# A four-layer residual chain whose instruction order is a table of numbers: the numbers of the prologue and of blocks 0 to 13 are replaced

## The chip, the cores and the metric

The kernel runs on one core of one Trainium2 chip. The time is device microseconds of one launch; a kernel is given as the median of its runs. A profiled execution also gives a span, from the first to the last instruction, and a trace of every instruction.

## The reference

The input x is 128 sequences of 64 tokens with 256 features. Four layers are added to it, one after the other, each steered by conditions of the sequence:

```
x = x + L0(x, cond)     # modulated linear, 16-head self-attention with q = k = v, modulated linear
x = x + L1(x, cond)     # per-sequence down projection, relu, up projection, plus its input
x = x + L2(x, ids ...)  # layer norms with gathered gains, small MLPs, a 6*256 -> 256 -> 256 MLP, layer norm
x = x + L3(x, cond)     # a rank-30 weight decoded per sequence: out = x @ (U V) + bias
```

In L0 the keys are `kx = x @ w_mod.T`, the scores `kx kx.T / 4` for each head, `A = softmax(scores)` and `out = A @ kx`. In L2 the first gain is gathered by a token's id out of 250 rows, the others out of 5 or 3 rows, and `_mlp_ln` is a silu MLP with a layer norm behind it. All of it is float32.

## The kernel before

**Tiling.** The 8192 tokens are cut into 16 blocks of 512 (8 sequences). A block runs through all four layers; within the attention it is worked in two pairs of 256 tokens (`pair_attention`), and elsewhere in four tiles of 128. A prologue makes what all blocks share: the style vectors and demodulations (L722, L734, L735, L743), the down and up conditions, the decoded weights `uu` (matmuls at L851, VectorE or ScalarE behind them at L866 and L858), the weights `w_t`, `w_s`, `w_h`, `w_x`, and the three small MLPs of L2 (the shared helper at L629 issues their matmuls).

**Order.** No loop sets the order of the instructions. Every operation is first noted with what it reads and writes (`Plan.op`), under its block (-1 for the prologue) and its running number in that block, counted from 0. `Plan.order` then emits them: of the operations whose predecessors are out and whose buffers are free it takes the one with the smallest number. The number is the block's start, 881500 times the block, plus an entry of the table `TURNS[block]`. Buffers of one kind are handed out in the order in which they were noted, except the four PSUM banks ("bank") and the one four-bank PSUM buffer ("sc"), which go to whoever comes first. So the tables alone set the order in the queues of TensorE, VectorE, ScalarE, GpSimd and SyncE, each of which runs strictly in the order it was given.

```
    def turns(blk, k):
        return max(blk, 0) * TURN + tables[blk][k]
...
    while plan.noted[-1] + 1 < SPINS:
        spin()
```

**Spins.** `SPINS` is the length of table -1. The prologue notes 231 operations; the rest of the table's entries are `spin`, a bf16 matmul of zeros into a bank that nobody reads (L638).

**The steps that are spoken of below**, with their entries in a block's table:

- 17 and 18 (GpSimd, L1097) scale x by the style; 19 to 22 are the gathers of gains, an indirect DMA each, issued from GpSimd (L1112).
- 31 and 59 (TensorE, L1191) are the key products of the two pairs, 8 matmuls of 128x256 each; VectorE multiplies them out (L1202) and GpSimd adds a bias (L1213).
- 34 to 62: VectorE transposes the keys (L1228, and L1245 for the values), ScalarE makes `kR` (L1237, entries 32 and 60), TensorE turns the values (L1256, entries 34 and 62).
- 36, 64 in block 0, and 40, 68 in the later ones: the scores (L1276), 128 small matmuls and 128 weight loads; they need `kR` and the buffer "sc". VectorE takes their maxima (L1289), TensorE subtracts them (L1350), ScalarE exponentiates (L1364).
- 48, 76 in block 0, and 52, 80 in the later ones: the results (L1381), again 128 small matmuls with 128 loads.
- L1418, L1155: the turn of the result and the output projection. L1573 and L1591: the down and up products. L1688: turns for the normalised x. L1738: the large MLP, 8 groups of matmuls of 128x512 for each half. L1785: the second MLP layer.
- In the prologue, entries 177 and 181 are the second and third of the MLPs' first products (L629), each for one half of the features.

**DMA.** Loads and stores are issued from SyncE's queue; a store or a load that reads what another engine has just made holds up every load behind it there.

Of the kernel before, what the change touches and what calls it, by code (L numbers as in the profile page):

```python
# [66 lines left out]
class Plan:  # L67
# [98 lines left out]
    -652225 -652207 -501809 -501797 549383 103302 97834 98988 -85347 -290328 36942 -280951 36928 -327022 -327038  # L166
    -295554 -34519 99192 -93568 76051 -488538 -331376 250663 -320110 311371 -544127 -297616 224193 -331358 437866
    369544 404601 258598 475097 427655 312750 413551 304934 313766 312765 477842 -325751 561445 451452 460137 631735
    653018 914561 435225 761948 708892 413433 313012 683513 477384 477856 415801 449087 706556 405021 840033 397966
    837121 677936 790176 413437 1085501 936816 1219990 374944 1127563 -488523 52290 364768 79632 -329221 31806 69353  # L170
    -302391 37394 74911 -302398 -135690 103317 253823 37375 113108 263257 -19093 -550935 407657 459732 455180 631946
    302035 554215 632190 302064 695445 435656 1285010 1313672 -271895 459095 641073 632445 439004 715974 662881
    443771 715988 735063 451708 763102 706553 455767 763114 790156 408270 1002127 1127290 1030643 1260783 1163421
    1039496 1260792 1322499 1326714 1592341 1603338 1296229 962570 1143817 400034 1095103 400034 1114596 1105723
    370540 1181851 589031 1073580 1215404 1215398 420508 1317621 426029 1244494 1155098 517782 411678 1318626
    1221030 487418 1289492 1063938 409314 1219811 414916 1426329 1505888 1316718 425996 578876 1307095 1544800
    1509955 1509945 1500478 1779993 1762953 1714110 1556735 1872029 1343778 1433951 1901071 1540726 1505870 1355549
    1749223 1065262 1886158 1894341 1920839 1713830 1294728 1463917 2023267 2025009 2024993 1769125 2080980 1991910
    1476886 1764730 2069423 1404270 2200384 1433935 1923896 1907021 2044892 1919551 2192488 1893429 2159446 1342047
    1346981 1402219 2313495 2045469 2494753 2285999 2271380 2543401 2525610 1728898 1728909 2630317 2592995 1746037  # L180
    2451743 1728921 2595973 1718576 1277644 2062908 2395255 316359 450207 16049267 16049281 14504150 -291503
    11290964 2389482 -291825 16049286 -291820 14522440 16049266 16053420 -320001 13567795 -410994 14513815 -361547
    15405911 16048186 16073369 -309973 14522440 16005249
    """,
    0: """
    -484581 84372 -652203 -35682 684863 1289506 1005368 578863 1258365 2419509 2111364 2061858 1597541 357479
    -327047 377451 733801 366553 -328204 806711 387288 365083 406034 1377907 1111313 1160718 1672215 -332266 56194
    404606 447219 455369 431572 -15187 267150 595783 567747 302041 312750 629212 662899 609068 653445 312737 466428
    715978 309121 309112 857128 436276 489161 370548 806701 1063944 1120732 641246 410676 725568 436305 410648
    709812 410662 609042 1119259 602370 436294 477217 820104 818673 1002143 818654 1083255 1103114 1063941 1120265  # L190
    1117581 1073560 1181852 1168792 409321 1262701 1205334 414910 1357801 1505886 426004 1063898 411662 1462748
    1518640 1230468 1433890 1749255 1749239 1431873 1872425 2190164 1919575 1872422 2174910 2278764 2321415 2384852
    2430654 2088493 2292286 2543835 2599889 2409496 1589520 2271367 2543830 2512135 1803634 1326310 2714126 1751071
    1758943 1758957 1758947 2523186 1589506 2427752 2206922 2711663 1788133 2711694 1788156 2575469 2528666 2544499
    2733360 2898539 2917556 2711682 2568763 2598822 2598852 2711679 2711696 2733311 2598849 2781651 2986041 2354176
    2409591 2568757 2598832 2711671 2711680 2733358 2733329 2733335 2985571 2986044 2476838 3049866 2529124 3019122
    3049851 2529112 3092405 3152898 3152886 2477574 3204028 3204039 2342116 2350219 3160743 3160731 2697860 3153889
    3310393 3353979 3296818 3367447 3109127 3394993 3420441 3762300 1336203 3409996 1469597
    """,
    1: """  # L200
    -394079 -394092 -482733 -425615 -297831 -337865 -325537 -299039 -482716 297196 735637 407985 -421370 1532404
    443756 1548772 1282128 -1264679 -1264697 916581 1275890 1398962 1806910 176525 220234 -35053 255915 516626
    953340 1101650 829819 -272447 -445206 -64857 -359383 -359389 244494 192909 345134 348760 345130 -367222 -461014
    348778 399333 182401 437115 -417743 -417760 535346 420908 265999 768088 829973 832612 837576 833713 675251
    992893 182426 -481464 -506569 -460994 -466571 450753 -394211 625417 462288 625425 618981 624383 413787 413768
    669870 343193 742774 770597 629993 403311 404542 576441 1104386 1135196 1129763 833262 576451 1171507 595405
    1281040 1289755 520725 1288546 1288527 1081797 1404289 982233 1509004 1472691 1546270 1619792 2137602 1717458
    880232 2135345 2272406 1286799 2320256 2356575 2322518 1460605 2544746 2443636 2180116 2356564 1460588 2544726
    2443622 2044761 2544726 2667741 2486731 2485304 2485318 2485298 2245174 2417516 2227520 2427513 2713637 2584615
    2732909 2598456 2420038 2515062 2444000 2464209 2891247 2903613 2544651 2550373 2576192 2608410 2732899 2803358  # L210
    2464175 2465276 2999349 3013321 2916210 2539226 2567809 2577443 2710725 2727178 2803374 2464189 2454008 2930134
    2862729 3001178 3086911 2483864 2483874 3086910 2483867 3104930 2787555 2777533 3153776 2867590 2867592 1986833
    3029354 2367123 2367108 1913805 2953463 3334225 3302746 3334216 3352156 3407259 3425296 3382877 3491141 471262
    3509343 449882
    """,
    2: """
    -506971 -506984 -473467 -51547 -995523 -772166 -1268595 -801997 -473451 -48533 -341685 -506980 -506979 -519158
    306888 -502791 1004205 -58852 -58870 589526 2052273 589554 1561323 -500303 35094 -350214 -59960 220156 325567
    197340 398256 -206237 108215 71820 160868 160862 187456 160866 -299085 267210 -360793 311626 281895 -319 304375
# [1800 lines left out]
```

## Time and profile before

| what | value |
|---|---|
| median of 9 runs | 822.09 us (817.21 to 828.91) |
| the profiled execution's own time | 822.83 us |
| its span | 821.1 us |
| mean granted TensorE clock | 0.982 |
| TensorE matmuls busy | 754.5 us (92%) |
| VectorE busy | 589.4 us (72%) |
| GpSimd busy | 565.6 us (69%) |
| ScalarE busy | 361.3 us (44%) |

The profiled execution is 1.7 us longer than its span and 0.7 us above the median of the runs. Busy times of an engine are sums over its instructions; the granted clock is the share of full speed that TensorE was given. An idle time is put down to what ended it: "DVE mr" is a VectorE instruction that wrote mr, "issue" means that the engine waited for nothing that the profile shows.

### The profile page before, as it was taken

The numbers are of one execution on the slowest core, as the hardware profiler recorded it, in microseconds if no ns is written. First come the engines' busy times: TensorE is split into PE (matmuls) and PEld (weight loads), VectorE is DVE, ScalarE is ACT, GpSimd is POOL, SyncE is SP. The second block draws the span as 40 slices with busy tenths as digits, with TensorE's granted clock in tenths as the row PEclk, the third lists the DMA queues.
The fourth block names the chain that finished last, engine by engine and source line by source line (L and its number), as shares of the span: only waits on it lengthen the run. The fifth ranks groups of instructions, "written<-read, shape, count | busy, mean of one in ns | idle before, by whom it ended". The sixth has DMA issues, their size and how long they took to land.

```text
span 821.1 us, 29440 instructions
## 1 busy us (share of the span) xinstructions
PE 754.5 (92%) x12839; PEld 489.8 (60%) x12843; DVE 589.4 (72%) x1320; ACT 361.3 (44%) x664; POOL 565.6 (69%) x544
## 2 busy tenths in 40 slices
PE   8778889999999999999999999999999989999695
PEld 6655655666666565666666665656566655655353
DVE  4747885967868696969687786869596876866435
ACT  1564345453536362544435353625355253444331
POOL 5453878395877878586869688795779586828243
PEclk9996999999999999999999999999999999999989
DMA  8776652234332234333433333342434232023001
GB/s 264 246 238 207 211 131 79 77 104 106 110 112 78 77 97 130 92 118 93 108 102 95 106 102 93 97 136 67 123 87 117 80 80 65 3 66 100 17 1 52
DMA packets 59297, 87.63 MB, mean 107 GB/s; under 512 B 6456, under 2 KB 42400, under 8 KB 59168
## 3 DMA queue, kind: packets, MB, share of 16 engines
q1 hardware_dynamic: 54048, 68.96, 28.7%
q0 software_dynamic: 5120, 16.78, 7.2%
q8 instruction: 101, 1.65, 0.9%
q14 instruction: 28, 0.23, 0.1%
HBM read 72.48 MB, written 13.24 MB: 104 GB/s over the span
## 4 chain that ended last, share of the span: by engine, by line
PE 60%; DVE 18%; POOL 8%; ACT 5%; issue 4%; DMA 4%; SPq 0%; DVEq 0%; POOLq 0%; ACTq 0%
PE bank L1738 23%; PE bank L1191 5%; PE bank L1785 5%; PE sc L1276 4%; DVE st L611 3%; PE bank L1688 3%; DVE mr L1289 3%; PE bank L1381 3%; PE bank L1155 2%; PE bank L629 2%; PE bank L1573 2%; PE bank L1591 1%; DVE bank L1162 1%; PE bank L1648 1%; PE bank L1823 1%
## 5 line engine op out<-in xcount | busy, mean ns | idle before, releaser
L1289 DVE TENSOR_REDUCE mr<-sc 128x16 f32<-128x1024 f32 x64 | 75.7, 1211 | 11.3 <-PE sc L1276 11.2
L1364 ACT ACTIVATE e<-sc 128x1024 f32<-128x1024 f32 x64 | 62.4, 1027 | 35.2 <-PE sc L1350 35.2
L1112 POOL DMA_INDIRECT pw<-in_pw,idx x64 | 65.3, 1021 | 16.0 <-issue 8.2
L1155 PE MATMUL bank<-osT,wo 128*128 128x512 f32 x128 | 63.8, 627 | 5.4 <-DVE osT L1425 5.1
L1191 PE MATMUL bank<-wk,xsT 128*128 128x256 f32 x256 | 62.1, 385 | 1.3 <-DVE uu L866 0.6
L1738 PE MATMUL bank<-uu,w_s 128*128 128x512 f32 x128 | 63.3, 597 | 0.0
L1237 ACT ACTIVATE kR<-kT,early 128x1024 f32<-128x1024 f32 x32 | 39.7, 1242 | 50.6 <-DVE kT L1228 50.6
L1738 PE MATMUL bank<-uu,w_t 128*128 128x512 f32 x128 | 61.3, 605 | 0.3 <-ACT uu L1655 0.2
L1738 PE MATMUL bank<-uu,w_h 128*128 128x512 f32 x128 | 61.4, 602 | 0.0
L1381 PEld LDWEIGHTS bank<-e,v 64*32 64x32 f32 x4096 | 45.0, 107 | 27.5 <-issue 23.4
L1276 PEld LDWEIGHTS sc<-kR,kT 20*64 20x64 f32 x4096 | 48.1, 132 | 20.5 <-ACT e L1364 8.2
L1738 PE MATMUL bank<-x2T,w_x 128*128 128x512 f32 x128 | 59.9, 593 | 0.0
L1381 PE MATMUL bank<-e,v 64*32 64x64 f32 x4096 | 52.5, 229 | 7.9 <-issue 7.7
L1785 PE MATMUL bank<-w,uu 128*128 128x256 f32 x240 | 55.8, 385 | 2.1 <-DVE uu L1758 2.0
L1276 PE MATMUL sc<-kR,kT 20*64 20x64 f32 x4096 | 53.2, 235 | 4.7 <-issue 1.9
L1191 PEld LDWEIGHTS bank<-wk,xsT 128*128 128x128 f32 x256 | 48.5, 196 | 12.7 <-issue 4.0
L1202 DVE TENSOR_TENSOR kxe<-bank,dmk 128x512 f32<-128x512 f32 x32 | 22.0, 688 | 44.2 <-PE bank L1191 38.6
L1693 ACT COPY uu<-bank 128x512 f32<-128x512 f32 x64 | 36.5, 587 | 38.6 <-PE bank L1688 38.4
L1129 POOL TENSOR_TENSOR wdn<-gdb,late 128x512 f32<-128x512 f32 x32 | 40.6, 1283 | 14.5 <-PE bank L1573 13.9
L1785 PEld LDWEIGHTS bank<-w,uu 128*128 128x128 f32 x240 | 44.3, 190 | 9.7 <-DVE uu L1758 4.0
L1228 DVE STREAM_TRANSPOSE kT<-kxe 128x512 f32<-128x512 f32 x64 | 42.1, 684 | 9.3 <-POOL kxe L1213 9.3
L1213 POOL TENSOR_TENSOR kxe<-kxe,kbr 128x512 f32<-128x512 f32 x32 | 41.0, 1282 | 11.0 <-DVE kxe L1202 10.7
(241 smaller groups left out, 1782.5 us busy)
## 6 DMA issues: line engine op xcount, KB each, us to landing
xT<-in_xT SPq DMA_DIRECT2D x32, 256.0 KB
gdb<-dgdb SPq DMA_DIRECT2D x16, 512.0 KB
ubb<-ugub SPq DMA_DIRECT2D x32, 256.0 KB
wup<-ugub SPq DMA_DIRECT2D x32, 256.0 KB
ids<-in_ids SPq DMA_DIRECT2D x16, 256.0 KB
ud<-uu SPq DMA_DIRECT2D x8, 512.0 KB
uT<-ud SPq DMA_DIRECT2D x16, 256.0 KB
dmk<-demod_k SPq DMA_DIRECT2D x60, 64.0 KB
```

The lines of the kernel that those rows point to most:

```text
L1112: lambda tl=tl, n=n: nc.gpsimd.indirect_dma_start(out=pw[tl // 2].t[:, tl % 2, :], out_offset=None, in_=a["pw"], in_offset=bass.IndirectOf ...
L1129: lambda w=w, dp=dp: nc.gpsimd.tensor_tensor(w(), gdb.t[:, :, 0:64], dp, ALU.mult),
L1155: nc.tensor.matmul(ps.t, owT[:, c, bass.ts(oc, 128)], osT.t[:, c, :], start=(c == 0), stop=(c == C - 1))
L1191: nc.tensor.matmul(ps.t[:, bass.ts(l, F)], xsT.t[:, c, mine2].rearrange("p (n l) -> p l n", l=2)[:, l, :], kwT[:, c, :], start=(c == 0), s ...
L1213: lambda: nc.gpsimd.tensor_tensor(kxe.t[:, :, :, 0:D], kxe.t[:, :, :, 0:D], heads(kinds["kbr"][0]).unsqueeze(1).to_broadcast([128, 2, H, D ...
L1228: lambda l=l: nc.vector.transpose(kT.t[:, l, :].rearrange("p (g h t) -> p h g t", h=H, t=QT), kxe.t[:, l, :, :]),
L1276: nc.tensor.matmul(sc.t[64 * c : 64 * c + 64, q, bass.ts(tg, 64)], cut(kT.t)[r, tg // 4, c, tg % 4, :], cut(kR.t)[r, tg // 4, c, tg % 4, : ...
L1289: lambda two=two: nc.vector.tensor_reduce(mr.t[:, two, :], sc.t[:, two, :].rearrange("p q (g n) -> p q g n", g=TG), AX.X, ALU.max),
L1364: lambda k=k: nc.scalar.activation(es[k].t, sc.t[:, 2 * k : 2 * k + 2, :], AF.Exp, scale=0.25),
L1381: nc.tensor.matmul(placed(pr[c].t)[32 * q : 32 * q + 32, l, g, :, :], v.t[r, l, :].rearrange("p (g q d) -> p g q d", g=4, q=4)[:, g, q, :] ...
L1738: lambda ps=ps, w=w, src=src, fc=fc, c=c, n=n: nc.tensor.matmul(ps.t, w.t[:, c, bass.ts(fc, 128)], src.t[:, c, :], start=(n == 0 and c == ...
L1785: nc.tensor.matmul(ps.t[:, bass.ts(l, F)], s2.t[:, c, bass.ts(2 * p + l, 128)], w2.t[:, c, :], start=(c == 0), stop=(c == C - 1),)
```

## The change

Only the tables change, and those of blocks 14 and 15 stay as they are. In tables -1 and 0, 200 of 254 and 160 of 184 numbers differ; in tables 1 to 13, between 171 and 186 of 188. Table -1 grows from 254 to 260 entries, so that 29 spins are issued where there were 23. All other operations are the same. The core of the diff, the rows that hold the entries spoken of below:

```
     -1: """
...
-    2451743 1728921 2595973 1718576 1277644 2062908 2395255 316359 450207 16049267 16049281 14504150 -291503
-    11290964 2389482 -291825 16049286 -291820 14522440 16049266 16053420 -320001 13567795 -410994 14513815 -361547
-    15405911 16048186 16073369 -309973 14522440 16005249
...
+    2622265 1775307 2426970 1697160 2571200 1682278 2026759 2026610 2358957 316359 458461 13107617 16049235 13742698
+    -291503 13107634 650263 -280935 16049248 -329374 16049263 16216606 16049220 -346953 16049242 -422713 16216620
+    -302053 15394192 16034132 14522442 -331757 16046838 16046865 3098908 3226051 11288552 14520045 16046827 16037492
     """,
     0: """
...
-    715978 309121 309112 857128 436276 489161 370548 806701 1063944 1120732 641246 410676 725568 436305 410648
-    709812 410662 609042 1119259 602370 436294 477217 820104 818673 1002143 818654 1083255 1103114 1063941 1120265
...
+    715978 670665 708898 841873 300921 300901 377359 796595 1080902 1128281 641217 312749 722185 518743 307513
+    557778 307531 708702 1112996 656157 387879 358903 768396 766965 950435 766946 1092590 1112449 1078881 1135205
...
     1: """
-    -394079 -394092 -482733 -425615 -297831 -337865 -325537 -299039 -482716 297196 735637 407985 -421370 1532404
-    443756 1548772 1282128 -1264679 -1264697 916581 1275890 1398962 1806910 176525 220234 -35053 255915 516626
-    953340 1101650 829819 -272447 -445206 -64857 -359383 -359389 244494 192909 345134 348760 345130 -367222 -461014
...
+    -475790 -480517 -480506 -439237 -295604 -295623 -306545 -306564 -481411 409304 726230 398578 374496 1282148
+    1193293 1161391 1209564 -129480 -147706 1078814 1094978 444778 1813295 177455 -504031 213695 -504015 806623
+    938402 1078729 -504036 -313003 -580569 -55894 -493636 -493638 231682 203755 355019 371081 346268 -494805 -494820
...
```

A number alone doesn't tell a place: an operation can't go before its predecessors, nor before the operation that takes the buffer ahead of it. Raised to the largest number among those, some entries stand so (TURN times the block included):

| block, entry | what | before | after |
|---|---|---|---|
| 0, 62 | TensorE turns the values, second pair | 725568 | 722185 |
| 0, 64 | scores, second pair | 725568 | 722185 |
| 1, 17 and 18 | GpSimd scales x | 487421 | 752020 |
| 1, 31 | keys, first pair | 641246 | 752020 |
| 1, 59 | keys, second pair | 1063926 | 752020 |
| 0, 48 | results, first pair | 857128 | 841873 |
| 7, 3 | VectorE makes the one-hot of the ids | 5956073 | 5465118 |
| 9, 17 | GpSimd scales x | 7788290 | 6280542 |

## The prediction

> **What bounds the kernel now.** I read the busy tenths first, then the busy time in stretches of 20 us, then fine stretches where the clock is below 1, then TensorE's timeline around its idle times. The first view has TensorE's busy tenths and its granted clock, a digit for each 20.5 us.
>
> ```profile
> PE   8778889999999999999999999999999989999695
> PEclk9996999999999999999999999999999999999989
> ```
>
> TensorE is full from the seventh slice to the thirty-sixth. It is loose at the start, where the prologue and blocks 0 and 1 run, and at the end, in block 15. The windows say by how much (start and end, length, then busy us and count of each engine, clock, DMA):
>
> ```profile
> core 0: us, PE busy (x) PEld busy (x) DVE busy (x) ACT busy (x) POOL busy (x), PEclk, DMA share, GB/s
> 0.00:20.00 20.00, 15.90 (x68) 12.06 (x69) 8.94 (x16) 2.45 (x4) 11.86 (x22) 1.00 0.85 264
> 20.00:40.00 20.00, 15.06 (x223) 12.72 (x222) 14.17 (x27) 9.75 (x22) 7.69 (x8) 1.00 0.78 244
> 40.00:60.00 20.00, 14.15 (x437) 11.19 (x438) 9.72 (x16) 14.32 (x35) 12.86 (x11) 1.00 0.80 258
> 60.00:80.00 20.00, 15.81 (x295) 11.21 (x298) 14.05 (x25) 9.51 (x22) 7.32 (x6) 0.66 0.63 192
> 80.00:100.00 20.00, 16.46 (x429) 12.76 (x419) 16.79 (x28) 6.63 (x15) 16.46 (x15) 0.91 0.70 215
> 100.00:120.00 20.00, 17.93 (x445) 13.01 (x444) 18.12 (x38) 6.66 (x13) 13.68 (x14) 1.00 0.52 136
> 120.00:140.00 20.00, 16.75 (x149) 10.60 (x150) 13.79 (x34) 11.25 (x23) 16.74 (x18) 0.91 0.33 84
> 140.00:160.00 20.00, 19.95 (x398) 12.56 (x400) 14.95 (x35) 7.58 (x14) 7.18 (x8) 1.00 0.29 85
> ```
>
> The first seven rows have 112.1 us of TensorE work in 140 us: 27.9 us idle. The four rows from 740 to 820 us hold 18.46, 11.99, 19.00 and 12.40, so 18.2 us are idle there; the orders of blocks 14 and 15 stay, and only spins come in. All rows together hold 754.5 us, which leaves 580.6 us of work for the 600 us between: 19.4 us idle, 3%. So there are three funds: 27.9 us early, 19.4 us spread over twelve blocks, 18.2 us late that the change hardly touches. TensorE sets the time throughout, since its work is fixed, and an order can gain only idle time and clock.
>
> **The clock.** Fine stretches of the same view:
>
> ```profile
> 60.00:62.50 2.50, 2.11 (x84) 1.79 (x88) 1.70 (x4) 0.67 (x2) 0.00 (x0) 0.63 0.42 147
> ...
> 72.50:75.00 2.50, 2.50 (x5) 0.98 (x4) 1.54 (x4) 2.14 (x6) 0.00 (x0) 0.64 0.18 46
> ...
> 95.00:97.50 2.50, 2.50 (x131) 1.82 (x129) 1.83 (x4) 0.00 (x0) 2.42 (x2) 0.50 0.52 193
> ...
> 122.50:125.00 2.50, 2.50 (x57) 2.11 (x40) 1.75 (x4) 0.25 (x2) 2.50 (x3) 0.50 0.05 14
> ```
>
> A clock of 0.63 over 2.5 us is half speed for 1.85 us of it, 0.64 is half speed for 1.8. So half speed lasts from 60.65 to 74.3 us, and, with the neighbours' 0.96 and 0.86, 0.92 and 0.90, also from 94.8 to 98.2 and from 122.1 to 125.5: 13.65, 3.4 and 3.4 us. TensorE is busy throughout the two short ones, so each costs 1.7 us. In the long one it is busy for some 11 us, so at most 5.5 us. What stands ahead of them is in TensorE's timeline (start, length, what, and in brackets the idle time before it):
>
> ```profile
> 40.82 1.59 PE L1276 MATMUL sc<-kR,kT 20*64 20x64 f32 x128 [1.09 <-ACT kR L1237]
> ...
> 46.83 1.12 PE L1381 MATMUL bank<-e,v 64*32 64x64 f32 x91 [1.45 <-issue]
> ...
> 60.39 0.31 PE L1381 MATMUL bank<-e,v 64*32 64x64 f32 x7 [2.14 <-issue]
> ...
> 93.70 0.49 PE L629 MATMUL bank<-p 64*128 64x128 f32 x2 [1.43 <-DVE kxe L1202]
> ...
> 121.79 1.42 PE L1381 MATMUL bank<-e,v 64*32 64x64 f32 x87 [1.91 <-issue]
> ```
>
> Waits of 2.14, 1.43 and 1.91 us end 0.3 to 1.1 us ahead of the three drops. Two of them, and the 1.45 us, stand inside a group of 128 small matmuls with nothing to wait for but "issue". I take that for the fetch of TensorE's own instructions, because it falls in groups with the most instructions per microsecond and while the DMA engines are busy. Over the whole run:
>
> ```profile
> PE bank L1381 <- issue: 7.7, 6, 2.1
> PE sc L1276 <- issue: 1.9, 2, 1.3
> ```
>
> **The change, part by part.** I sorted the table's numbers, each raised to those of its predecessors and of the operation that takes the buffer ahead. It leaves out when banks and "sc" come free, so a shift of one or two places in it is not certain. Counted as pairs that change places, TensorE has 270, ScalarE 85, VectorE 323, GpSimd 918, SyncE 2310: long moves are those of loads, gathers (1021 ns each) and one-hots that were early anyway; the compute order changes locally. On SyncE block 1's two loads of x pass three others, 0.43 us of issue each (the one at 19.54 us); nothing early waits for what they pass, so I cost that at nothing, and at 1.3 us if one of the three is the decoded weights' load that TensorE waits for.
>
> 1. *First score group of block 0's second pair.* Its values (62) and scores (64) now precede block 1's keys (31), and the keys of block 1's second pair (59) follow these. Before, the keys ran from 37.83 to 39.73 and covered most of the wait for kR (ScalarE's 39.50 to 40.76, behind two exponentials). With 0.66 us of values (L1256) as the only cover from 38.0 us, the wait is 40.82 - 38.0 - 0.66 = 2.2 us in place of 1.09: **+1.1**. The scaling of block 1 (17 and 18, 2.04 us on GpSimd at 33.4) now stands behind the bias add of L1213, which can start 1 us earlier, at no gain, since kR waits for ScalarE.
> 2. *The results of that stretch (48)* then have two key products (3.8 us) and two small groups between them and the scores. That spreads the instructions, and I expect the 1.45 us wait to go: **-1.45** (bounds 0 and -1.45).
> 3. *Block 2's second scores (68)* go ahead of a prologue product (entry 209, L629, 1.13 us at 113.31) that covered their wait for the exponentials (they end at 115.4): **+1.0**. The product, block 3's keys and the value turns (66) now stand between these scores and the results at 119.22, so the 1.91 us wait should go: **-1.9** (bounds 0 and -1.9).
> 4. *The third small MLP's second product* (181, at 93.70) waited for a bank. Its raised number hardly moves (1540726 to 1568303), and a sort doesn't show banks: half of 1.43, **-0.7** (bounds 0 and -1.43).
> 5. *Clock.* With the 1.91 us wait the half-speed stretch at 122.1 goes, -1.7; with half of the other, -0.85: **-2.6**. The long stretch stays: the results and scores around 60.39 keep their order. Bounds: all three go, -8.9; or one more long stretch comes, +4.8 (TensorE is busy 14.15 of 20 us at 40 to 60, so 9.7 of 13.65 us, half of which is lost).
> 6. *Six more spins.* Back to back at full clock they run at 1.45 us for 6 (at 807.71), 0.24 each. The code counts 20000 to the microsecond; by that about five fall into full stretches (two near 155 to 161 us, three near 655 to 690) where there was one: 4 x 0.24 = **+1.0**. The rest stand in waits at the start and the end; without that cover they add 0.5.
> 7. *Blocks 2 to 13.* Pairs of dense groups with nothing between them fall from 10 to 8 in the sorted numbers. The waits there are short (0.3 to 1.0 us: L1688 for VectorE's ao, L1155 for osT, and four fetches of 0.65 to 1.0). VectorE's and GpSimd's moves hide behind TensorE (they are busy 589.4 and 565.6 of 821 us); a gather moved ahead of a bias add would hold the keys by its 1.02 us if that cover were gone. I take **-1.2**, the fifth of the 3.3 us of fetches and half a microsecond of the rest; bounds, a third of the 19.4 us either way, -6.5 and +6.5.
>
> Sum: 1.1 - 1.45 - 1.9 + 1.0 - 0.7 - 2.6 + 1.0 - 1.2 = -4.75. The span of 821.1 becomes 816.3. The profiled execution took 822.83, 0.74 above the median, so I take the sum off the median: 822.09 - 4.75 = **817.3 us**. The fastest run of before, 817.21, says the same from another side: this order gives it when its waits and the clock fall well.
>
> A rule that speaks against the change: the Trainium skill, "TensorE: Matmul & The Clock Gate", section "What's actually happening", calls the cost of the clock's ramp below 1% of a typical span, different from run to run with the phase of a free-running window, and not to be fitted to. The rows above show 20.5 us of half speed after short waits. By the rule the clock term would be 0 and the result 819.9 us.
>
> **Rivals.** *The waits come back as others.* VectorE is busy 18.12 of 20 us at 100 to 120 and 16.79 before, GpSimd 16.46 and 16.74 in two rows, so what TensorE gains there it may spend waiting for them. Then the covers lost (+2.1), the spins (+1.0) and the fetches gained (-3.4) nearly cancel, and the clock gives one short stretch: -2.0, **820 us**. For it: eight of ten dense pairs stay. Against: at 40 to 60 and 120 to 140 VectorE has 9.72 and 13.79 only.
>
> *Slower: a new half-speed stretch at 38 us.* The wait of 2.2 us in step 1 is longer than the 1.43 and 1.91 that stood ahead of drops, and as long as the 2.14. If it trips the clock for a long stretch, that costs 4.8, with the covers 2.1 and the spins 1.0: +7.9, **830 us**. It decides from a wait of about 2 us; for it, that the three drops of the trace follow such waits; against, that 2.14 us at 5.2 to 7.4 us were followed by a clock of 1.00, and that a spin was put near 32 us.
>
> **How the numbers follow.** Chances: forecast 0.49, waits that come back 0.28, slower 0.23. About 0.5%, 4.1 us, is what a measurement of this kernel can tell from no change: faster is below 818.0, slower above 826.2. The forecast's own range is 811 to 819. For the whole, below 808 (the long stretch gone too, 817.3 - 5.5 = 811.8, and most of the bound of step 7) I leave 0.06, above 828 a good half of the slower case, 0.13: 808 to 828.
>
> **What would show it.** Right: 24 us or less of idle TensorE in the first 140, no wait above 1 us inside L1381 near 45 and 120 us, clock 1.00 at 120 to 140. Wrong in step 1: the wait for kR at 40 us stays near 1 us. Wrong in step 5: half-speed stretches at other places with the same sum. The prediction falls if TensorE's idle time between 140 and 740 us moves by more than 4 us, or if fetch waits turn up at new places.

## The result, and the profile after

| | before | after |
|---|---|---|
| median, runs taken side by side | 823.9 us (62 runs, 817.21 to 834.0) | 831.1 us (20 runs, 828.58 to 835.56) |
| profiled execution, its span | 822.83, 821.1 us | 829.46, 827.7 us |
| mean granted clock of the profiled execution | 0.982 | 0.978 |
| start of block 0's large MLP (L1738 before, L1739 after) | 132.5 us | 139.7 us |
| start of block 12's large MLP | 673.0 us | 679.8 us |

The new order is slower: the ratio is 1.0097, with a 95% interval of 1.0077 to 1.0117. Ratios leave disturbed runs out and medians do not, so the two can differ by a few tenths of a per cent. Lines of the changed kernel have numbers one higher than before.

The whole loss is there when block 0 reaches its large MLP: +7.2 us. From there to block 12's both kernels take the same time (540.5 and 540.1 us), and at the end of the span the difference is 6.6. The busy tenths of TensorE and its granted clock, a digit for each 20.7 us, show the place: TensorE has lost a tenth in the third to fifth slices and in the seventh, the clock is now lowered a little in the third and fourth slices and not in the fourth alone, and from the eighth slice on TensorE is as full as before.

```profile
PE   8767788999999999999999999999999989999696
PEclk9988999999999999999999999999999999999989
```

Cut exactly at that mark, the windows give (start and end, length, then busy us and count of TensorE's matmuls, weight loads, VectorE, ScalarE, GpSimd; clock; DMA), first for before, then for after:

```profile
0.00:132.51 132.51, 104.58 (x2003) 80.13 (x2005) 89.88 (x162) 58.45 (x124) 80.54 (x86) 0.92 0.68 205
```

```profile
0.00:139.73 139.73, 107.12 (x2004) 82.55 (x2005) 91.74 (x162) 58.50 (x124) 78.11 (x83) 0.90 0.62 193
```

The same matmuls are behind both, but for one record. TensorE's idle time rose from 27.9 to 32.6 us, +4.7, and the work took 2.5 us longer: 4.7 + 2.5 = 7.2. Most of the 2.5 is the granted clock: TensorE was busy for 18.3 us of before's half-speed stretches and for 22.4 us of after's, and half of that difference, 2.1 us, is lost by it. A second pair of traces (before_c and after_c below, with the mark at 132.06 and 139.55 us) has 5.9 us of idle time and 1.6 us of longer work, so idle time is the larger part in both pairs. The trace's clock records begin at 12.9 us; from there to 140 us they have half speed in these stretches (start, length in us):

| kernel | half speed from 12.9 to 140 us | sum |
|---|---|---|
| before | 60.64 (13.65), 94.78 (3.41), 122.08 (3.41) | 20.5 |
| after | 16.34 (3.41), 29.99 (3.41), 43.64 (6.83), 70.95 (6.83), 88.02 (3.41), 125.56 (3.41) | 27.3 |

TensorE's timeline around these places (start, length, what, and in brackets the idle time before it) has the answers to the lines shown of before:

```profile
16.59 3.45 PE L1192 MATMUL bank<-wk,xsT 128*128 128x256 f32 x8
...
45.89 2.26 PE L1277 MATMUL sc<-kR,kT 20*64 20x64 f32 x128 [5.30 <-ACT kR L1238]
...
54.44 1.48 PE L1382 MATMUL bank<-e,v 64*32 64x64 f32 x128
...
68.47 0.31 PE L1382 MATMUL bank<-e,v 64*32 64x64 f32 x7 [1.16 <-issue]
73.57 0.49 PE L1277 MATMUL sc<-kR,kT 20*64 20x64 f32 x9 [2.93 <-issue]
124.93 1.23 PE L1277 MATMUL sc<-kR,kT 20*64 20x64 f32 x77 [1.49 <-issue]
129.42 1.49 PE L1382 MATMUL bank<-e,v 64*32 64x64 f32 x128
```

The wait for kR grew from 1.09 to 5.30 us. The results at 54.44 and 129.42 run through, 128 matmuls without a gap: the fetch waits of 1.45 and 1.91 us that stood there are gone. Others of 2.93 and 1.49 us stand in score groups, where the longest of before was 1.3. "Fetch waits" are the waits for "issue" inside these groups of 128, as in the prediction. The sums of waits in after (us in total, times, longest):

```profile
PE sc L1277 <- ACT kR L1238: 5.3, 1, 5.3
PE sc L1277 <- issue: 5.0, 4, 2.9
PE bank L1382 <- issue: 2.4, 3, 1.2
```

Before, the two fetch sums were 7.7 + 1.9 = 9.6 us; now they are 7.4.

**What the fetch waits are.** The prediction only argued that TensorE waits there for its own instructions; the traces show it. The profile has a queue of instructions, in both kernels alike:

```profile
q8 instruction: 101, 1.65, 0.9%
```

Its 101 packets have 16,384 bytes each, and TensorE's 25,836 recorded instructions in before (matmuls, weight loads and semaphores) are 101 times 256, but for 20. In before the fetch waits of 0.25 us or more stand at instructions 450, 962, 1473, 1730, 3777, 11457, 16320 and 23232: always whole multiples of 256 apart, to within 2, whatever operation is there. Each ends 1.2 to 1.6 us after a packet has landed. Over all eighteen traces, up to 760 us, 70 of the 79 waits of 0.8 us or more inside these groups stand at such places, the new ones of 2.93 and 1.49 us among them. So an order changes which operation stands there and how early the packet lands: at the place of the 1.45 us (instruction 962) it landed 1.5 us ahead in before and 6.2 us ahead in after.

**Why kR is late.** kR (ScalarE) needs kT (VectorE's transposes). VectorE's timeline of after:

```profile
38.95 3.75 DVE L811 TENSOR_SCALAR wsm<-wsm 128x6 f32<-128x6 f32 x1
42.62 0.70 DVE L1246 STREAM_TRANSPOSE kV<-kxe 128x512 f32<-128x512 f32 x1
43.25 1.25 DVE L1229 STREAM_TRANSPOSE kT<-kxe 128x512 f32<-128x512 f32 x2
```

and of before:

```profile
36.27 0.45 DVE L810 TENSOR_SCALAR wsm<-wsm 128x6 f32<-128x6 f32 x1
36.72 0.71 DVE L1245 STREAM_TRANSPOSE kV<-kxe 128x512 f32<-128x512 f32 x1
```

The first instruction scales six columns, weights of the prologue that are not needed until w_t is made. It shows 3.75 us in one kernel and 0.45 in the other. The transposes that lead to kR stand behind it in VectorE's queue and start as it ends (42.62 us). GpSimd's timeline of after at that time:

```profile
38.40 0.98 POOL L1113 DMA_INDIRECT pw<-in_pw,idx  x1
39.40 2.05 POOL L1098 TENSOR_TENSOR xsT<-xT,style_k 128x512 f32<-128x512 f32 x2
41.40 1.26 POOL L1130 TENSOR_TENSOR wdn<-gdb,late 128x512 f32<-128x512 f32 x1
42.74 1.27 POOL L1136 TENSOR_TENSOR wdn<-wdn,gdb 128x512 f32<-128x512 f32 x1
```

and of before:

```profile
33.41 2.04 POOL L1097 TENSOR_TENSOR xsT<-xT,style_k 128x512 f32<-128x512 f32 x2 [9.60 <-PE bank L1191]
35.41 1.27 POOL L1213 TENSOR_TENSOR kxe<-kxe,kbr 128x512 f32<-128x512 f32 x1
36.83 0.99 POOL L1112 DMA_INDIRECT pw<-in_pw,idx  x1
```

In after, GpSimd's multiplications follow one another without a gap from 39.40 to 42.66, and VectorE's small instruction ends at 42.70. In before GpSimd had the scaling of x (xsT) behind it when wsm came; only the bias add was running, which ended at 36.68, and wsm ended at 36.72. So the scaling of x, moved behind the bias add (17 and 18 in the prediction's step 1), now runs exactly when VectorE wants to start wsm. The experiments test that reading.

### The profile page after: what moved, and what is told of

It is laid out like the page before. It is cut to its first block, busy times and chain, and to the rows that moved or that the text cites. A ratio compares the mean times of both kernels' runs of the same rounds, so it can differ in the third digit from the quotient of the medians.

```text
span 827.7 us, 29465 instructions
## 1 busy us (share of the span) xinstructions
PE 758.2 (92%) x12841; PEld 491.9 (59%) x12849; DVE 591.8 (72%) x1320; ACT 360.4 (44%) x664; POOL 567.0 (69%) x544
## 4 chain that ended last, share of the span: by engine, by line
PE 63%; DVE 19%; POOL 8%; ACT 5%; issue 4%; DVEq 0%; POOLq 0%; ACTq 0%
PE bank L1739 23%; PE bank L1192 6%; PE sc L1277 4%; PE bank L1786 4%; DVE st L612 3%; PE bank L1689 3%; PE bank L1382 3%; PE bank L1156 2%; PE bank L630 2%; DVE mr L1290 2%; PE bank L852 2%; DVE ao L1395 2%; PE bank L1574 1%; DVE uu L1759 1%; PE bank L1649 1%
## 5 line engine op out<-in xcount | busy, mean ns | idle before, releaser
L1290 DVE TENSOR_REDUCE mr<-sc 128x16 f32<-128x1024 f32 x64 | 75.7, 1211 | 12.9 <-PE sc L1277 12.9
L1192 PE MATMUL bank<-wk,xsT 128*128 128x256 f32 x256 | 66.4, 406 | 1.1 <-DVE mE L1338 0.8
L1739 PE MATMUL bank<-uu,w_s 128*128 128x512 f32 x128 | 64.0, 600 | 0.0
L1739 PE MATMUL bank<-uu,w_t 128*128 128x512 f32 x128 | 62.0, 607 | 0.0
L1739 PE MATMUL bank<-uu,w_h 128*128 128x512 f32 x128 | 60.9, 601 | 0.0
L1739 PE MATMUL bank<-x2T,w_x 128*128 128x512 f32 x128 | 60.7, 594 | 0.0
L1192 PEld LDWEIGHTS bank<-wk,xsT 128*128 128x128 f32 x256 | 51.1, 208 | 14.1 <-issue 4.4
L1382 PE MATMUL bank<-e,v 64*32 64x64 f32 x4096 | 49.9, 226 | 2.6 <-issue 2.4
```

The costliest lines, as they stand in the source:

```text
L1192: nc.tensor.matmul(ps.t[:, bass.ts(l, F)], xsT.t[:, c, mine2].rearrange("p (n l) -> p l n", l=2)[:, l, :], kwT[:, c, :], start=(c == 0), s ...
L1290: lambda two=two: nc.vector.tensor_reduce(mr.t[:, two, :], sc.t[:, two, :].rearrange("p q (g n) -> p q g n", g=TG), AX.X, ALU.max),
L1382: nc.tensor.matmul(placed(pr[c].t)[32 * q : 32 * q + 32, l, g, :, :], v.t[r, l, :].rearrange("p (g q d) -> p g q d", g=4, q=4)[:, g, q, :] ...
L1739: lambda ps=ps, w=w, src=src, fc=fc, c=c, n=n: nc.tensor.matmul(ps.t, w.t[:, c, bass.ts(fc, 128)], src.t[:, c, :], start=(n == 0 and c == ...
```

## The experiments

All were timed in rounds beside the kernel before on the same chip. In two of the four sessions before took 831 to 832 us, in the other two 824 to 825, so ratios and marks are compared, not times. A mark is the start of a block's large MLP. Block 0's is at 132.5 and 132.1 us in two traces of before and at 139.7 and 139.5 in two of after, but at 133.9 and 131.7 in f_cde and f2_cde, and at 144.3 and 140.6 in g_stall and j_step1 (all four below); each of these pairs has one order. So a mark that moves by 3 us says little by itself; the waits given with it carry the reading. Each edit changes numbers of the tables alone; what is given is the change of order that results. In the kernels with edited tables the line numbers are 3 to 5 lower than before's.

### Halves of the change

*Front alone* takes tables -1, 0 and 1 from the change; *rest alone* takes tables 2 to 13.

```
a_front: TURNS = new tables -1, 0, 1 and old 2 to 13
b_rest:  TURNS = old tables -1, 0, 1 and new 2 to 13
```

> Tables -1, 0 and 1 of the changed kernel (so 29 spins), tables 2 to 13 of the one before. Theory A, the loss is made in the first 60 us: the whole of it shows, ratio to the kernel before 1.008 to 1.012, and at 80 us the work stands some 8 us behind. Rival B, the loss is made in blocks 2 to 13: ratio 0.998 to 1.002. Rival C, each half bears a part: near 1.005.

> The other half: tables -1, 0 and 1 of the kernel before (23 spins), tables 2 to 13 of the changed one. Theory A: ratio 0.997 to 1.003, as TensorE has only 19.4 us of idle time in those blocks and the order there changes by a place or two. Rival B: 1.008 to 1.012. Rival C: near 1.005.

Measured: front alone 1.0076 (1.0039 to 1.0112), so the front by itself makes a loss of the size of the whole. But rest alone is slower too, 1.0089 (1.0056 to 1.0122), which was not expected. Its trace falls 1 to 3 us behind before's up to 95 us and is level again at block 2's first scores (101.90 us, before 101.92). Then this stands on VectorE's timeline:

```profile
104.76 1.29 DVE L1224 STREAM_TRANSPOSE kT<-kxe 128x512 f32<-128x512 f32 x2
105.98 1.19 DVE L1285 TENSOR_REDUCE mr<-sc 128x16 f32<-128x1024 f32 x1
107.09 0.68 DVE L1421 TENSOR_TENSOR osT<-bank,style_o 128x512 f32<-128x512 f32 x1
```

and on TensorE's:

```profile
107.82 6.55 PE L1151 MATMUL bank<-osT,wo 128*128 128x512 f32 x8 [2.26 <-DVE osT L1421]
```

Block 2's transposes and a maximum go ahead of the 0.68 us that block 1's output projection waits for. Its eight matmuls start after a wait of 2.26 us and take 6.55 us, at half speed; in before they wait 0.89 and take 3.70. To see whether that is the cause, one VectorE instruction (osT) was put back ahead of them:

```
 h_os: b_rest with table 2
-entries 41, 62, 63: 286788 272821 286776
+entries 41, 62, 63: 311626 304978 -476973
```

> The mixed kernel with the old prologue and blocks 0 and 1 and the new blocks 2 to 13 (1.0089), with one VectorE instruction put back: osT of block 1 ahead of block 2's key transposes and maximum. Theory (its loss comes from that delay, the 2.26 us wait and the half speed behind it): the wait ahead of the output product near 108 us is about 0.9 us, the half-speed stretch at 106.8 us is gone, the ratio falls to 1.001 to 1.005. Rival (blocks 2 to 13 themselves are slower in the new order): the wait shrinks but the ratio stays at 1.007 to 1.010.

Measured: the same product on TensorE's timeline,

```profile
104.90 3.70 PE L1151 MATMUL bank<-osT,wo 128*128 128x512 f32 x8 [0.85 <-DVE osT L1421]
```

so the wait is down to that of before, no half-speed stretch falls on the product, and the ratio is 1.0059 (1.0027 to 1.009). The wait alone doesn't decide the clock: in c_wsm below the same product waits 0.85 us as well and takes 5.40, since a stretch begins at 108.69 us. The point value fell by 0.003 and lies outside what the theory had (up to 1.005) and outside the rival's 1.007; the intervals overlap. The marks say more: block 0's large MLP starts at 136.8 us instead of before's 132.5. Half-speed stretches at 120.5 and 130.8 us and a fetch wait of 1.33 us stand between. So the half of the tables from block 2 on does no good with the old front either, and 4 to 5 us are lost by block 0's mark. Whether the steady blocks bear a part, these traces can't tell: from block 0's mark to block 12's before takes 540.5 us, this run 542.1, rest alone 545.2 and front alone, whose tables are old there, 547.4; but g_stall and j_step1 below, of one order, take 546.5 and 539.5. The losses of the halves don't add up to that of the whole: in after, where the front is 7 us later, the same product waits only 0.85 us (at 112.30) and takes 3.70.

With block 2's table left old as well:

```
h_b2: TURNS = old tables -1 to 2 and new 3 to 13
```

> The kernel before with the new order in blocks 3 to 13 alone (tables of the prologue and of blocks 0, 1 and 2 as before). Theory (the loss is made where the prologue still runs): 0.999 to 1.002. The prediction's step 7: -1.2 us for blocks 2 to 13, 0.9985. Rival (the new order of the steady blocks costs time, as the 1.0059 with one repair suggests): 1.004 to 1.008.

Measured: medians 824.79 against 824.46, ratio 1.0038 (1.0005 to 1.0072); block 0's large MLP to block 12's takes 539.6 us, before 540.5. The ratio lies between the theory (up to 1.002) and the rival (from 1.004), nearer the rival; the medians and the trace go with no loss in the steady blocks. It is open to a few tenths of a per cent; a gain it is not.

### The wait for kR

Scaling of wsm moved behind the transposes and maxima, in the changed kernel:

```
 c_wsm: after with table -1
-entry 56: 383051
+entry 56: 722190
```

> The changed kernel with one number of table -1 changed (entry 56), so that VectorE's scaling of the 6 mixing weights stands behind the three key transposes and the maxima of block 0's second pair and not ahead of them. Theory A1: that instruction took 3.75 us in the changed kernel because it waited for GpSimd's unbroken run, and all of it went into the wait for kR (5.30 us). Then the wait for kR falls to about 2.2 us, bounded by the exponentials on ScalarE, and the time falls by some 3 us: ratio to the kernel before near 1.006. Rival A2: the loss is the clock's, and the order of a 6-column instruction is worth nothing: ratio stays 1.009 to 1.010.

Measured: wsm takes 0.22 us, the wait for kR falls from 5.3 to 2.8, block 0's large MLP starts 3.2 us earlier (136.5); ratio 1.0037 (1.0007 to 1.0067).

Then the other side: the kernel before, with the scaling of x behind the bias add and a gather, and nothing else but scores 64 ahead of keys 31 that follows from it:

```
 g_stall: before with table 1
-entries 17, 18: -1264679 -1264697
+entries 17, 18: -129480 -147706
```

> The kernel before with only block 1's numbers 17 and 18 (scaling of x on GpSimd) taken from the change: the bias add and a gather go ahead of them, as the prediction's step 1 has it, and the scores 64 ahead of the keys 31. Theory: VectorE's six-column scaling of wsm now waits for GpSimd's unbroken run, 2 us or more instead of 0.45; the wait for kR is 2.5 to 5 us in place of 1.09; ratio 1.002 to 1.007. The prediction's step 1: the wait for kR is 2.2 us, wsm stays below 0.5 us, +1.1 us, ratio 1.001. Rival (in the order of before there is cover enough): no change, 0.999 to 1.001.

Measured: 1.0109 (1.0064 to 1.0153), more than the whole change. VectorE, GpSimd and TensorE in its trace:

```profile
39.43 7.63 DVE L805 TENSOR_SCALAR wsm<-wsm 128x6 f32<-128x6 f32 x1
```

```profile
40.12 2.04 POOL L1092 TENSOR_TENSOR xsT<-xT,style_k 128x512 f32<-128x512 f32 x2
42.12 2.48 POOL L1124 TENSOR_TENSOR wdn<-gdb,late 128x512 f32<-128x512 f32 x2
44.56 2.47 POOL L1130 TENSOR_TENSOR wdn<-wdn,gdb 128x512 f32<-128x512 f32 x2
```

```profile
50.25 2.26 PE L1271 MATMUL sc<-kR,kT 20*64 20x64 f32 x128 [9.09 <-ACT kR L1232]
```

GpSimd ends at 47.03, VectorE's six columns at 47.06. The run was longer here than in after: the multiplications of wdn stand two and two and follow without a gap, where after's alternate and leave 0.08 us. The wait for kR is 9.1 us, well past the theory's 2.5 to 5.

The next edit was meant to move wsm in this kernel, but the number given (722190 in entry 56 of table -1) left the order as it was, so the run repeats g_stall in another session:

> The kernel before with block 1's 17 and 18 taken from the change (the run of 1.0109), and VectorE's six-column scaling of wsm moved behind the transposes and the maxima. Theory (nothing but the held VectorE makes that run slow): wsm back to 0.2 to 0.5 us, the wait for kR from 9.1 to about 1.1 to 2.2 us, ratio 0.999 to 1.003. The prediction's step 1: wait 2.2 us, +1.1 us, 1.001. Rival (the late scaling of x and the clock of that order): the wait goes, the ratio stays above 1.005.

Measured: 1.0119 (1.0064 to 1.0174), wsm 7.63 us and the wait 9.09 again, to the hundredth. It says nothing on the theories' difference. With a number that does move it, one VectorE instruction apart from g_stall:

```
 l_late: g_stall with table -1
-entry 56: 415801
+entry 56: 740000
```

> The kernel before with block 1's 17 and 18 taken from the change (1.0109 and, run again, 1.0119), and now truly with VectorE's scaling of wsm moved behind the two maxima: one VectorE instruction against that run. Theory (the slow run is the held VectorE and what follows from it): wsm 0.2 to 0.5 us, the wait for kR from 9.1 to 1.1 to 2.2 us, the 140 us mark back from 141 to 144 us to at most 135, ratio 0.999 to 1.004. The prediction's step 1: wait 2.2 us, +1.1 us. Rival (late scaling of x and its clock): the wait goes, the ratio stays above 1.006.

Measured: 1.0021 (0.9989 to 1.0052), block 0's large MLP at 133.5 us. VectorE and TensorE:

```profile
44.53 0.22 DVE L805 TENSOR_SCALAR wsm<-wsm 128x6 f32<-128x6 f32 x1
```

```profile
40.55 1.60 PE L1271 MATMUL sc<-kR,kT 20*64 20x64 f32 x128 [2.83 <-ACT kR L1232]
```

One small instruction, 0.22 us of work, makes the difference between 1.011 and 1.002, whose intervals don't overlap. What is left of the wait, 2.83 us, is the lost cover that the prediction's step 1 spoke of (2.2); the rival's ratio, above 1.006, lies outside the interval. In the changed kernel, with wsm in the change's place, the scaling of x was put back, and block 1's keys with it, the first pair's ahead of the scores:

```
 e_keys: after with table 1
-entries 17, 18, 31, 59: -129480 -147706 -313003 -174909
+entries 17, 18, 31, 59: -1264679 -1264697 -272447 182426
```

> The changed kernel with four numbers of block 1 put back (17, 18, 31, 59): xsT ahead of the bias add on GpSimd, keys 31 ahead of scores 64, all else as in the change; wsm stays where the change has it. Theory (17 and 18 behind the bias add make the wait for kR): wait 5.3 to about 1.1 us, the 140 us mark about 3 us earlier than the changed kernel's 139.7, ratio 1.001 to 1.005. Rival (wsm's place alone makes it): the wait stays at 3 us or more, ratio as the changed kernel's, 1.005 to 1.010.

Measured: wsm 0.23 us, wait 1.09 us, block 0's large MLP at 136.4 us, 3.3 earlier than after; ratio 1.0044 (1.0014 to 1.0074). So either order alone, x early or wsm late, ends the hold; the keys that cover the wait again make the rest of the difference between 1.09 us here and 2.8 in c_wsm.

### The first keys

The change moves the second demodulation product (two matmuls of 8x256, at 17.05 us in before) ahead of block 0's first keys. In the changed kernel it was put back; in the kernel before it was moved to where the change has it:

```
 d_dmk: after with table -1
-entry 23: -327069
+entry 23: -320110
 k_dmk: before with table -1
-entry 23: -320110
+entry 23: -700000
```

> The changed kernel with one number of table -1 changed (entry 23), so that the second demodulation product goes back behind block 0's first keys. Theory A3: the product ahead of the keys costs 0.46 us of wait and 0.69 us of work, and its 8 rows with the waits around it drop the clock at 16.3 us, which doubles the keys' 1.9 us: the keys start at 15.3 to 15.5 us, the half-speed stretch at 16.3 us goes, and the time falls by 2 to 3 us, ratio near 1.007. Rival: what is gained at 16 us is lost in the wait for VectorE's kV at 22 us, ratio stays 1.009 to 1.010.

> The kernel before with one TensorE product moved: the second demodulation product goes ahead of the first one's follower and of block 0's first keys, as in the change. Theory (it delays the keys past the point where the clock drops): keys at about 16.6 us instead of 15.2, lasting 3.4 us instead of 1.9, half speed from 16.3 us, first scores 2 us later, ratio 1.002 to 1.005. Rival (the clock there is chance): keys later by 1.2 us, no half speed, ratio 0.999 to 1.002.

Measured: back in place 1.0039 (1.0004 to 1.0073), moved in before 1.004 (1.0002 to 1.0077). TensorE with it back,

```profile
14.74 1.90 PE L1188 MATMUL bank<-wk,xsT 128*128 128x256 f32 x8
```

and with it moved in the kernel before:

```profile
16.50 3.58 PE L1186 MATMUL bank<-wk,xsT 128*128 128x256 f32 x8
```

Moved, the keys start 1.3 us later than before's 15.22 and run at half speed from 16.5 us; the first scores come at 27.4 instead of 25.8 us. With it back, the stretch at 16.3 us is gone and the first scores come at 25.3. The other traces agree: in all seven with the product moved, half speed begins at 15.9 to 16.5 us and the first scores come at 27.4 to 28.0; of the eleven others only g_stall has half speed there (16.18, first scores 28.8), and the first scores of the other ten come at 24.8 to 27.0.

### All three put back, and the marks

```
f_cde, f2_cde: after with the edits of c_wsm, d_dmk and e_keys
after_c:       after itself
before_c:      before itself
```

> The changed kernel with three local orders put back: the second demodulation product behind block 0's first keys; VectorE's scaling of wsm behind the transposes and maxima; and in block 1 the scaling of x (17, 18) ahead of the bias add on GpSimd, with keys 31 ahead of scores 64. Theory (the loss is a few named waits in the first 60 us, and they add): the wait for kR falls from 5.3 to about 1 us, first scores near 25.3 us, the 140 us mark 6 us earlier than the changed kernel's, ratio 0.998 to 1.003. Rival (the clock's phase decides, and a single edit wins by shifting it): the waits go, but half-speed stretches turn up elsewhere, and the ratio stays at 1.004 to 1.008.

> The run with the three local orders put back once more, on another chip, since 1.0017 [0.998, 1.005] leaves open whether anything of the loss remains. Theory (three orders are the whole of it): 0.998 to 1.002. Rival (the clock and the twelve blocks keep a part): 1.003 to 1.006.

Measured: 1.0017 (0.9981 to 1.0054) and, in another session, 1.0019 (0.9983 to 1.0054), medians 832.61 against 831.68 and 823.81 against 825.39. Block 0's large MLP starts at 133.9 and 131.7 us, where before has 132.5 and after 139.7: the loss up to there is gone. Two runs agree that nothing that can be measured is left; that a thousandth or two remains is not excluded. Nor is there any gain, though the wait for kR is as in before. TensorE in the second:

```profile
40.16 1.59 PE L1273 MATMUL sc<-kR,kT 20*64 20x64 f32 x128 [1.09 <-ACT kR L1234]
...
65.70 0.49 PE L1273 MATMUL sc<-kR,kT 20*64 20x64 f32 x9 [4.23 <-issue]
```

A fetch wait of 4.23 us in the last nine matmuls of a score group has taken the place of those that the change removed.

> The changed kernel itself, unaltered, as the mark for the other three on the same chip. Both theories: 1.008 to 1.012 of before, the wait for kR near 46 us about 5.3 us, the first keys near 16.6 us taking about 3.4 us. A ratio below 1.006 would say that part of the loss hangs on the chip and that the two single edits (1.0037 and 1.0039) bought less than they seem to.

Measured: 1.0048 (1.0016 to 1.008), with the keys at 16.9 us and a kR wait of 4.1, as wsm took 2.54 us here. The size of the loss differs between sessions, 1.005 to 1.010, so the single edits of c_wsm and d_dmk (1.0037, 1.0039) are shown to help by their traces, and only weakly by their times.

> The kernel before itself, for a trace on the chip of these runs, where it takes some 831 us instead of 823. Theory (half of the loss seen at first was the good clock that the old order had on the first chip): the marks up to 140 us stay within 2 us of those of the first trace, except for one or two more half-speed stretches, and the rest of the 8 us is lost to the clock at 720 to 830 us. Rival: new waits in the head of the kernel, 4 us or more by the 140 us mark.

Measured, one execution: 828.51 us, in a session where before's median was 824.46. Its marks stay within 0.5 us of the first trace's from block 0's to block 8's large MLP (488.9 and 489.3 us), and then it loses 5 us in one place. TensorE's timeline there,

```profile
672.74 0.42 PE L1381 MATMUL bank<-e,v 64*32 64x64 f32 x3 [3.92 <-issue]
```

and the same three matmuls in the first trace of before:

```profile
670.20 0.30 PE L1381 MATMUL bank<-e,v 64*32 64x64 f32 x3 [0.89 <-issue]
```

A fetch wait of 0.89 us became one of 3.92, and 6.83 us of half speed began within it, at 671.9. Such places may be part of why runs of one kernel differ by 1 to 2%. It is not what the theory had (the clock at 720 to 830 us), and the rival's new waits in the head did not show either.

### The spins

```
 i_spin: after with table -1
-five entries: 650263 3098908 3226051 13107617 13107634
```

> The changed kernel without five of its spins: the one near 32 us, two near 155 to 161 us, two near 655 us; 24 spins are left where before has 23. The prediction's step 6: 1.0 us less than the changed kernel, so 1.004 to 1.009 with the changed kernel at 1.005 to 1.010, and no other change. Rival (the spins hold the clock): more half-speed stretches between 32 and 60 us or at 160 us, ratio 1.010 or more.

Measured: 1.0071 (1.0042 to 1.0099), between the changed kernel's 1.0048 and 1.0097. Up to 46 us its times are those of after, so the spin near 32 us shows no effect: the stretch at 43.6 us comes with it and without. A microsecond either way is below what these runs tell.

## Why the prediction was wrong

The forecast was -4.75 us; the result is +7.2 in the medians and +6.6 in the spans. The likeliest case was wrong, and the slower rival (830 us, a wait for kR of 2 us or more that trips the clock at 38 us) came closest, in place and in size. Its own terms were not the real ones: it had a long half-speed stretch for 4.8 us and covers for 2.1, and the trace has 4.7 us of idle time and 2.5 of longer work. That its 830 us lies so near 831.1 is in part luck. One of the two arguments against it was a misreading: "2.14 us at 5.2 to 7.4 us were followed by a clock of 1.00". The views count time without a clock record as full speed, and before's records begin at 12.86 us. Ahead of that the matmuls themselves tell the clock: those of L851 start 0.21 us apart from 9.24 to 12.87 us and 0.11 us apart right behind it, as they do inside and behind the stretch that f_cde's records have at 7.30 us. So TensorE ran at half speed after that wait.

**The step that failed is step 1**, in its sentence that the scaling of x "now stands behind the bias add of L1213, which can start 1 us earlier, at no gain, since kR waits for ScalarE". It followed kR only to ScalarE's exponentials. It did not ask what runs on VectorE while the moved GpSimd work runs. VectorE's wsm was held 3.75 us by it, and the wait became 5.30 us, where the step had 2.2. Its +1.1 measured +4.2. The lost cover alone was judged well: 2.83 us when the hold is taken away (l_late). The cost missed is thus 5.30 - 2.8 = 2.5 us of idle time in the changed kernel, and 6.3 us (9.09 - 2.83) where the swap is made alone.

**Missing from the sum altogether:** the second demodulation product ahead of the first keys. The product takes 0.69 us, and it and the next one wait 0.46 us each for ScalarE (dmk), where before only one did. So the keys start at 16.59 us, 1.37 later, and fall into half speed. First scores 2 us later (27.8 instead of 25.8) are the price in the profiled executions; d_dmk and k_dmk show it from both sides.

**Steps 2 and 3** named waits that did go, those of 1.45 and 1.91 us. In step 2 one key product stands between scores and results where the step had two; the other comes behind the results (60.38). In step 3 the sorted numbers did not give TensorE's order: the prologue's last such product before the scores still stands ahead of them (121.58), and only block 3's keys stand between them and the results, as before. So the step's +1.0 did not come, and its wait moved, to 1.49 us in the scores. The steps counted the waits as gained, and all fetch waits in the two groups fell only from 9.6 to 7.4 us, -2.2 where -3.35 was forecast: the instruction packets still arrive late, at other operations. New waits stand in other groups (2.93 at 73.57, 1.49 at 124.93). The sum is no steady size either: 12.3 us in the trace of f_cde and 7.0 in that of f2_cde, one and the same program.

**Step 5**, the clock, had the wrong sign: -2.6 forecast, +2.1 to +2.5 found up to 140 us. By size this is the largest miss, some 5 us of the 12 between forecast and result. The long stretch did go, which was only a bound of the step, but six short ones came, one of them from within the 5.30 us wait (43.64, 6.83 us) and one at the keys (16.34). How much of the clock's loss comes of the longer waits the runs do not separate.

**Step 4** came out as taken: the 1.43 us ahead of that product are gone, but 0.48 us stand ahead of the next one (101.67), and the wait ahead of the one before it grew from 0.50 to 0.70, which leaves -0.75 where -0.7 was taken. **Step 6**, +1.0 for six spins, is inside the noise of i_spin. **Step 7**, -1.2 for blocks 2 to 13, was right that little happens there: -0.4 us between the large MLPs of blocks 0 and 12. Its bound of 6.5 either way is about what single executions of one order differ by there (7.0 us between g_stall and j_step1), and block 2 by itself, which overlaps the prologue, can lose as much: rest alone lost 6 us between its scores at 102 us and those at 121.

**The rule weighed in the prediction.** The Trainium skill, "TensorE: Matmul & The Clock Gate", section "What's actually happening", says that the activity window is free-running, so that the ramp differs from run to run, and costs below 1% of a typical span. The two traces of before agree that it differs: 20.5 us of half speed between 12.9 and 140 us in each, but at 60.64, 94.78 and 122.08 us in one and at 60.92, 77.99 and 91.64 in the other. The 1% is reached in mid-kernel alone: half of the 18.3 us that TensorE was busy in these stretches of before is 9.2 us, 1.1% of the span. What the change added, 2.5 us at most, is 0.3%, and a third of the result: too large to set to 0 where 0.5% is asked.

## What to carry to other kernels

When GpSimd work is moved in time, read what VectorE has to run at that time, and what stands behind it in VectorE's queue: here a six-column instruction of no urgency was held for as long as GpSimd kept busy, and the critical transposes stood behind it. Where half a per cent is at stake, a reordering is judged first where engines are loose, here the first 140 us; there one late instruction of 0.2 us can cost ten times its length, and then the clock adds to it. A fetch wait removed from one group of small matmuls is not a gain until the sum over all groups has fallen, since the next packet of instructions can be late at another operation.

## What was not expected of the hardware

- **VectorE held by GpSimd for several instructions on end.** The same `TENSOR_SCALAR` of 128x6 took 0.22 us with GpSimd idle, and 0.45 (before), 2.54 (after_c), 3.75 (after) and 7.63 us (g_stall); in these four it ended 0.03 to 0.04 us after a GpSimd instruction that a gap followed. Gaps of 0.06 us (after_c, 41.68 to 41.74), 0.08 us (after, 42.66 to 42.74) and 0.15 us (before, 36.68 to 36.83) let it in; one of 0.02 us (after, 39.38 to 39.40) did not, and the run of g_stall shows no gap above 0.02 us until 47.03. The transposes beside it kept their 0.70 and 1.25 us. The Trainium skill, "SBUF — State Buffer", section "Who interferes with whom", says that a tensor_scalar can enter a mode that uses two ports, that VectorE in such a mode contends with GpSimd for the port pair that they share, and that whoever is second blocks for the other's whole instruction. Which mode was used no trace here shows. The traces agree that the instruction waits for GpSimd and then ends at once; that one instruction is the longest hold is not so here: in after four GpSimd instructions in a row went first (a gather, two scalings of x and one multiplication of wdn), in g_stall seven.
- **Half speed comes in whole steps.** All stretches away from the end are 3.41, 6.83, 10.24, 13.65 or, in g_stall, 17.07 us, and in each trace they start whole multiples of 3.41 us apart. Where one falls on the eight matmuls of block 1's output projection, these take up to 6.55 us (b_rest) in place of 3.70.
- **TensorE can wait for its own instructions, at places 256 or a multiple apart.** Up to 4.2 us were seen (e_keys, f_cde, f2_cde), and each wait at such a place ended 1.1 to 1.6 us behind the landing of a 16,384-byte packet. The size varies between executions of one program: 0.89 and 3.92 us at the same three matmuls of before (instruction 23232).
